# A message-passing layer on one core: PE one iteration free of ACT's evictions, and gathers that wait for the weights eight batches back

## The chip, the cores and the metric

The kernel runs on one core of one Trainium2 chip. The metric is the time of one execution on the device in microseconds (us). The engines are named as in the profile: PE (TensorE, matmuls), DVE (VectorE), ACT (ScalarE), POOL (GpSimd, which here issues the gathers) and SP (SyncE, which issues plain transfers). They run side by side and wait for each other by semaphores. SBUF is the memory that the engines work in, PSUM the banks that PE writes into.

## The reference

One layer of a graph network over 12500 nodes of 160 numbers (64 scalars and 32 vectors of three) and 400000 edges, which are sorted by their target node:

```python
h = jnp.maximum(_layernorm(x), 0.0)
s0, s1 = linear maps of h, times node_vec1          # the node's own part
y0, y1 = linear maps of h, times node_vec1          # what edges fetch
w = silu(edge_attr_16 @ fc_W1 / 4) @ fc_W2 / 8      # 192 weights of each edge: w_a, w_b, w_c, w_d
ys0, ys1 = y0[edge_src], y1[edge_src]               # the gather
e0, e1 = edge_attr_4[:, :1], edge_attr_4[:, 1:]
mid_a = w_a * ys0 * e0
mid_d = w_d * einsum('euc,ec->eu', ys1, e1) / sqrt(3)
mid_b = (w_b * ys0)[:, :, None] * e1[:, None, :]
mid_c = (w_c * e0)[:, :, None] * ys1
z = zeros.at[edge_dst].add(concatenated mids)       # 384 numbers of a node
out = x + C_S * s + C_X * (linear maps of z, times node_vec1)
```

## The kernel before, in words

A node phase of some 280 us computes s (into `acc`, which stays in SBUF) and y (written to `y_d` in HBM). Then come the edges, in 3125 tiles of 128, four tiles to a batch: 782 batches. This main loop is the rest of the time, and the change is in it.

The work on one batch, with its lines in the profile of the kernel before:

- `load`: POOL issues four indirect gathers (L540), one for each tile, that bring 128 rows of `y_d` each into one of nine buffers `yg`. The row numbers stand in `src_sb`. For 22 of the batches (every 32nd up to 704) no rows are gathered: `made_...` computes them from x, in small steps spread over the iterations before. So 760 batches are gathered, in 3037 instructions.
- `hidden` (every second batch): PE multiplies the edges' inputs into a bank `px` (L550), and ACT takes them out through Silu into `hT` (L555).
- `weigh`: PE's four fp32 matmuls write the batch's weights into one of two PSUM slots `pw` (L566); behind them ACT copies three numbers of each edge into the same slot (L567). This copy waits for the matmuls.
- `lift_rows`: ACT multiplies the fetched rows by e0 into `yge` (L484, four times).
- `dots_of` and `products`: DVE forms `tmp` (L489, L491), `both` (L495) and the product tile `pr` (L496, L497, L500, L501). L495 is the last to read the fetched rows on DVE. A `pw` slot is free for the batch after next when L501 has read it.
- `select` (once for 12 tiles): DVE compares a row of 0 to 127, kept in the free end of a bank `pz`, with the edges' targets, into the one-hot tile `sel` (L583).
- `sums`: PE adds sel^T pr of each tile (L603) into one of two banks `pz`.

Tiles form 185 groups, of 24 tiles in the first 1824 tiles and of 12 after. At a group's end ACT takes the sums out (`zs`, L609), PE transposes them into a `px` bank (`turn`, L617), ACT takes that out (`za`, L621), PE multiplies by the last weights (`map_sums`, L630), ACT takes that out (`os`, L634 and L635), and DVE adds it into `acc` (`accumulate`, L645 and L648).

PE, ACT and DVE run their instructions in exactly the order in which the program writes them; each takes the next only when what it waits for is there, and whatever stands behind it waits too. POOL has a queue of its own, also in program order, and so has SP. One iteration b of the loop writes: load(b+8), weigh(b+2), the evictions that PE's work of earlier iterations left for ACT, lift(b+2), dots and products of b+1, select, accumulate, sums(b), turn and map of groups due, and hidden. A turn is due one iteration after its group's last batch e, a map two, an accumulate four. A gather into a `yg` buffer may start when DVE and ACT have read the batch nine back, which had the buffer before.

Of the kernel before, what the change touches and what calls it, by code (L numbers as in the profile page):

```python
# [28 lines left out]
WN = 128  # L29
TG = 12  # L30
EG = 8
WIDE = 3, 5
GN = 8
HN = 2
RB = 22
RS = 32
# [7 lines left out]
def kernel(  # L44
# [56 lines left out]
    nr = max(0, min(RB, (NB - 1) // RS - 1))  # L101
# [3 lines left out]
    def made(b):  # L105

        return b // RS - 1 if b % RS == 0 and 0 < b <= nr * RS else None

# [26 lines left out]
    ygp = ctx.enter_context(tc.tile_pool(name="yg", bufs=9))  # L135
# [172 lines left out]
    with (  # L308
# [21 lines left out]
        def find_x():  # L330

            of = src_sb[:, RS * GT:RS * GT * (nr + 1)].rearrange("p (r c) -> p r c", c=RS * GT)[:, :, 0:GT]
            whole = nrp.tile([P, nr, GT], I32, name="whole")
            nc.vector.tensor_scalar(whole, of, 7, None, ALU.arith_shift_right)
            nc.vector.tensor_copy(hi_f.rearrange("p (r c) -> p r c", c=GT), whole)
            nc.vector.tensor_copy(lo_f.rearrange("p (r c) -> p r c", c=GT), of)
            nc.vector.scalar_tensor_tensor(lo_f, hi_f, -float(P), lo_f, op0=ALU.mult, op1=ALU.add)

        def gather_x(lo, hi):

            for r in range(lo, hi):
                xr = nrx.tile([P, GT * D + 1], F32, name="xr")
                for k in range(GT):
                    c = (r + 1) * RS * GT + k
# [141 lines left out]
    def dot(tmp, wt, yg, n):  # L486

        y1 = yg[:, :n, M0:].rearrange("p t (c u) -> p t c u", c=3)
        nc.vector.tensor_tensor(tmp[:, :n, 0:3, :], y1, wt[:, :n, NW:NW + 3].unsqueeze(3).to_broadcast([P, n, 3, M1]),  # L489
                                ALU.mult)  # L490
        nc.vector.tensor_reduce(tmp[:, :n, 3, :], tmp[:, :n, 0:3, :].rearrange("p t c u -> p t u c"), AX.X, ALU.add)  # L491

    def multiply(pr, both, tmp, wt, yg, yge, n):

        nc.vector.tensor_mul(both[:, :n, :], wt[:, :n, 96:160], yg[:, :n, 0:M0])  # L495
# [9 lines left out]
    with (  # L505
# [5 lines left out]
        tc.tile_pool(name="made", bufs=2) as mk,  # L511
        tc.tile_pool(name="banks", bufs=1, space=PSUM) as banks,
    ):
        (hids, rows, lifted, dots, wts, sels, z_ps, z_sb, zT, o_sb, prs) = ({} for _ in range(11))
        leaving = []
# [10 lines left out]
        AHEAD = 8  # L526
# [3 lines left out]

        def load(b):
            load_xe(b * GT // BT)
# [6 lines left out]
            for k, t in enumerate(tiles_of(b)):  # L539
                nc.gpsimd.indirect_dma_start(  # L540
                    out=yg[:, k, :], out_offset=None, in_=y_d,
                    in_offset=bass.IndirectOffsetOnAxis(ap=src_sb[:, t:t + 1], axis=0))
# [36 lines left out]
        def select(u, pz):  # L579
# [3 lines left out]
            nc.vector.tensor_tensor(sels[u][:, 0:n, :], pz[:, ZC:].unsqueeze(1).to_broadcast([P, n, WN]),  # L583
                                    drel[:, u * TG:u * TG + n].unsqueeze(2).to_broadcast([P, n, WN]), ALU.is_equal)
# [364 lines left out]
```

## Time and profile before

| What | Value |
|---|---|
| median of 3 runs | 5222.7 us (5202.25 to 5230.44) |
| profiled execution, its own time | 5204.84 us |
| its span in the profile | 5203.0 us |
| granted PE clock, share of full speed | 0.857 |

The profiled execution took 1.84 us beside its span. All times of single instructions come from it. In the views a line such as L540 is line 540 of the kernel; a name such as `yg<-y_d` is what an instruction writes and reads; a wait names the instruction that ended it, which is "issue" where the profile sees none.

### The profile page before, as it was taken

Reading aid. Unit: us, or ns where it says so; the run is one execution under the profiler, and the core shown is the slowest. Engines: PE = TensorE matmul, PEld = TensorE weight load, DVE = VectorE, ACT = ScalarE, POOL = GpSimd, SP = SyncE. Lnnn points to the kernel's source line nnn. Section 1 sums busy time; section 2 is a strip of 40 time slices with the busy share of each in tenths; the row PEclk is TensorE's granted clock in tenths of the full one; section 3 lists DMA queues with packets and bytes.
Section 4 is the critical chain, followed back from the end, with each engine's and each line's share of the span. In section 5 each row is a group of like instructions: output and inputs, shape, how many; then the busy total and the mean of one; then the engine's idle time right before and its main releaser. Section 6 shows DMA issues by size and latency. Waiting matters only on the chain. (4 is left out here: it accounts for less than half of the span.)

```text
span 5203.0 us, 55078 instructions
## 1 busy us (share of the span) xinstructions
PE 4180.4 (80%) x16329; PEld 2384.2 (46%) x16329; DVE 3441.9 (66%) x7529; ACT 1764.7 (34%) x5580; POOL 2959.6 (57%) x3137
## 2 busy tenths in 40 slices
PE   4478888787888888888888878888888888888888
PEld 3334444444444444444444444444444444544444
DVE  4456667666666666776666666676767666766667
ACT  3323333333333333332333333333333333333333
POOL 4455655555555555555555555555555555655553
PEclk7778888888888888888888888888888888888888
DMA  5322222222222222222222222222222222232222
GB/s 180 115 57 58 61 58 62 58 60 60 57 60 59 60 61 57 59 61 60 57 60 58 60 57 57 60 60 58 60 54 61 58 59 57 61 94 57 57 57 58
DMA packets 227720, 333.84 MB, mean 64 GB/s; under 512 B 54714, under 2 KB 171526, under 8 KB 227158
## 3 DMA queue, kind: packets, MB, share of 16 engines
q0 software_dynamic: 150000, 256.20, 19.9%
q1 hardware_dynamic: 63618, 65.63, 4.0%
q10 hardware_dynamic: 13796, 8.44, 0.5%
q8 instruction: 130, 2.13, 0.2%
q14 instruction: 176, 1.44, 0.1%
HBM read 306.83 MB, written 23.22 MB: 63 GB/s over the span
## 5 line engine op out<-in xcount | busy, mean ns | idle before, releaser
L540 POOL DMA_INDIRECT yg<-y_d,src_sb x3037 | 2871.3, 945 | 2115.7 <-ACT yge L484 784.9
L603 PE MATMUL pz<-pr,sel 128*128 128x384 f32 x6250 | 2510.0, 548 | 58.4 <-issue 54.7
L603 PEld LDWEIGHTS pz<-pr,sel 128*128 128x128 f32 x6250 | 1259.2, 212 | 1032.0 <-issue 491.5
L489 DVE TENSOR_TENSOR tmp<-yg,pw 128x384 f32<-128x384 f32 x760 | 418.6, 551 | 1523.1 <-ACT pw L567 1292.7
L567 ACT ACTIVATE pw<-raw 128x12 f32<-128x12 f32 x782 | 141.9, 182 | 3289.3 <-issue 2801.2
L484 ACT ACTIVATE yge<-yg,raw 128x160 f32<-128x160 f32 x3037 | 1044.0, 421 | 0.0
L566 PE MATMUL pw<-w,hT 64*128 64x192 f32 x6250 | 839.5, 392 | 73.7 <-issue 24.1
L566 PEld LDWEIGHTS pw<-w,hT 64*128 64x128 f32 x6250 | 572.6, 212 | 545.1 <-issue 313.4
L497 DVE TENSOR_TENSOR pr<-both,pw 128x768 f32<-128x768 f32 x782 | 737.9, 944 | 0.0
L550 PE MATMUL px<-xe,w 32*128 32x512 f32 x782 | 522.9, 756 | 189.4 <-ACT os L635 137.1
L491 DVE TENSOR_REDUCE tmp<-tmp 128x128 f32<-128x384 f32 x782 | 464.1, 594 | 26.9
L583 DVE TENSOR_TENSOR sel<-pz,drel 128x1536 f32<-128x1536 f32 (+1 forms) x261 | 455.2, 1744 | 0.0
L501 DVE TENSOR_TENSOR pr<-pw,yge 128x384 f32<-128x384 f32 x782 | 428.0, 547 | 0.0
L617 PE MATMUL px<-ident,zs 128*128 128x128 f32 x555 | 112.7, 319 | 358.9 <-ACT zs L609 341.3
L500 DVE TENSOR_TENSOR pr<-pw,yge 128x256 f32<-128x256 f32 x782 | 326.6, 418 | 13.0 <-ACT yge L484 12.3
L495 DVE TENSOR_TENSOR both<-pw,yg 128x256 f32<-128x256 f32 x760 | 314.8, 414 | 0.0
L550 PEld LDWEIGHTS px<-xe,w 32*128 32x128 f32 x782 | 130.7, 209 | 345.5 <-ACT os L635 163.4
L630 PE MATMUL px<-wc,za 128*128 128x96 f32 x1110 | 165.5, 289 | 145.3 <-ACT za L621 137.7
L617 PEld LDWEIGHTS px<-ident,zs 128*128 128x128 f32 x555 | 74.2, 159 | 446.9 <-ACT zs L609 395.9
L630 PEld LDWEIGHTS px<-wc,za 128*128 128x128 f32 x1110 | 161.5, 205 | 207.4 <-ACT za L621 155.1
L555 ACT ACTIVATE hT<-px 128x512 f32<-128x512 f32 x391 | 229.3, 587 | 1.9 <-PE px L550 1.7
L496 DVE TENSOR_TENSOR pr<-pw,tmp 128x128 f32<-128x128 f32 x782 | 219.4, 281 | 0.0
(118 smaller groups left out, 1739.2 us busy)
## 6 DMA issues: line engine op xcount, KB each, us to landing
yg<-y_d,src_sb POOLq DMA_INDIRECT x3037
xe<-in_e SPq DMA_DIRECT2D x196, 128.0 KB
y_d<-ys ACTq DMA_DIRECT2D x12, 640.0 KB
xr_d<-xr SPq DMA_DIRECT2D x22, 320.5 KB
acc<-in_x SPq DMA_DIRECT2D x11, 640.0 KB
xm<-xr_d SPq DMA_DIRECT2D x22, 320.0 KB
out<-acc SPq DMA_DIRECT2D x11, 640.0 KB
raw<-in_e SPq DMA_DIRECT2D x32, 192.0 KB
```

Source lines behind the costliest of these rows:

```text
L484: nc.scalar.activation(yge[:, k, :], yg[:, k, :], AF.Copy, scale=e4v[:, k, 0:1])
L489: nc.vector.tensor_tensor(tmp[:, :n, 0:3, :], y1, wt[:, :n, NW:NW + 3].unsqueeze(3).to_broadcast([P, n, 3, M1]), ALU.mult)
L491: nc.vector.tensor_reduce(tmp[:, :n, 3, :], tmp[:, :n, 0:3, :].rearrange("p t c u -> p t u c"), AX.X, ALU.add)
L497: nc.vector.tensor_mul(pr[:, :n, 192:ZC].rearrange("p t (c u) -> p t c u", c=3), both[:, :n, :].unsqueeze(2).to_broadcast([P, n, 3, M0]), ...
L500: nc.vector.tensor_mul(pr[:, :n, 0:M0], wt[:, :n, 0:M0], yge[:, :n, 0:M0])
L501: nc.vector.tensor_mul(pr[:, :n, 96:192].rearrange("p t (c u) -> p t c u", c=3), wt[:, :n, M0:96].unsqueeze(2).to_broadcast([P, n, 3, M1]) ...
L540: nc.gpsimd.indirect_dma_start(out=yg[:, k, :], out_offset=None, in_=y_d, in_offset=bass.IndirectOffsetOnAxis(ap=src_sb[:, t:t + 1], axis=0))
L550: nc.tensor.matmul(ph, w1[r, :], xe[r, :], start=True, stop=True)
L566: nc.tensor.matmul(pw[:, k, 0:NW], hT[r, o:o + P], w2[r, :], start=True, stop=True)
L583: nc.vector.tensor_tensor(sels[u][:, 0:n, :], pz[:, ZC:].unsqueeze(1).to_broadcast([P, n, WN]), drel[:, u * TG:u * TG + n].unsqueeze(2).to ...
L603: nc.tensor.matmul(z_ps[g], sels[t // TG][:, t % TG, :], pr[:, k, :], start=first, stop=last)
L630: nc.tensor.matmul(px[:, lo:hi], za[:, k, :], wc[:, k, lo:hi], start=k == 0, stop=k == 1)
```

## The change

1. A group's turn is due two iterations after its last batch, its map two or three after the turn (so that it falls on an odd iteration, while `hidden` uses a `px` bank on even ones), and its accumulate two after the map. The transposes go into the group's own `pz` bank instead of a `px` bank. At iteration b PE then needs only what ACT took out in iteration b-1, and a `px` bank is used at most once in an iteration.
2. The row of 0 to 127 for `select` is kept in four pieces of 32 in the free columns 224 to 255 of the `pw` slots, no longer in `pz`. `select` stands ahead of the products of its iteration, behind the dots.
3. `both` moves from `products` into `dots_of`, ahead of the reduction.
4. A new step `name_rows`: ACT copies the four row numbers of batch b+10 into a small tile `ids` (12 buffers), right behind the copy into `pw` of batch b+2. The gathers read `ids`; so those of batch j stand behind the weights of batch j-8. The gathers are written at the end of the iteration, ten batches ahead, and nine batches before the loop instead of eight. SP's load of edge inputs comes two batches earlier.
5. The 22 batches whose rows are computed lie elsewhere: every 24th in the part of wide groups (16), every 48th after (6), with the steps spaced 6 or 12 iterations apart.

On PE, about a third through its program, the end of a group and what follows it. `L603`/`L623` are the sums, `L566`/`L582` the weights of a batch; `L566` of the second list is `hidden`, and `L689`/`L709` belong to a computed batch. Before:

```order
L603 MATMUL pz_1673<-pr,sel 128x384 x4
L689 MATMUL px_1676<-ident,m_h 128x128 x2
L689 MATMUL px_1676<-ident,m_oh 128x128
L566 MATMUL pw_1671<-w_99,hT 128x192 x4
L603 MATMUL pz_1674<-pr,sel 128x384 x4
L617 MATMUL px_1675<-ident,zs 128x128 x3
L550 MATMUL px_1676<-xe,w_98 128x512
L566 MATMUL pw_1672<-w_99,hT 128x192 x4
L603 MATMUL pz_1674<-pr,sel 128x384 x4
L630 MATMUL px_1675<-wc,za 128x96
```

After:

```order
L623 MATMUL pz_1679<-pr,sel 128x384 x4
L709 MATMUL px_1681<-ident,m_h 128x128 x2
L709 MATMUL px_1681<-ident,m_oh 128x128
L582 MATMUL pw_1676<-w_99,hT 128x192 x4
L623 MATMUL pz_1678<-pr,sel 128x384 x4
L566 MATMUL px_1680<-xe,w_98 128x512
L582 MATMUL pw_1677<-w_99,hT 128x192 x4
L623 MATMUL pz_1678<-pr,sel 128x384 x4
L637 MATMUL pz_1679<-ident,zs 128x128 x3
```

The transposes of a group (L617, now L637) stood ahead of the second batch of weights behind the group's end, and now stand behind it and the sums that follow it. They write `pz_1679`, the group's own bank; before it was a `px` bank, whose other one `hidden` took right behind.

On ACT, also at the end of a group: the copy into `pw` (L567, now L583) and what stands behind it. Before:

```order
L567 ACTIVATE pw_1671<-raw 128x4x3
L609 ACTIVATE zs<-pz_1673 128x384
L693 ACTIVATE m_t<-px_1676 128x384
L484 ACTIVATE yge<-yg,raw 128x160 x4
L567 ACTIVATE pw_1672<-raw 128x4x3
```

After (L545 is the copy of row numbers):

```order
L583 ACTIVATE pw_1676<-raw 128x4x3
L545 ACTIVATE ids<-src_sb 128x4
L629 ACTIVATE zs<-pz_1678 128x384
L713 ACTIVATE m_t<-px_1681 128x384
L493 ACTIVATE yge<-yg,raw 128x160 x4
L583 ACTIVATE pw_1677<-raw 128x4x3
```

Behind each copy into `pw` there is now the copy of row numbers, ahead of the evictions and the lifts.

On POOL, in the middle of its program, a batch's four gathers and the first of the next, with the semaphores that each waits for. Before:

```order
L540 DMA yg<-y_d,src_sb 128x160 [waits DMASW0_49,DVE_49,Activation_49]
L540 DMA yg<-y_d,src_sb 128x160 [waits DMASW1_49]
L540 DMA yg<-y_d,src_sb 128x160 [waits DMASW2_49]
L540 DMA yg<-y_d,src_sb 128x160 [waits DMASW3_49]
L540 DMA yg<-y_d,src_sb 128x160 [waits DMASW4_49,DVE_49,Activation_49]
```

After:

```order
L555 DMA yg<-y_d,ids 128x160 [waits DMASW0_49,DVE_49,Activation_49]
L555 DMA yg<-y_d,ids 128x160 [waits DMASW1_49]
L555 DMA yg<-y_d,ids 128x160 [waits DMASW2_49]
L555 DMA yg<-y_d,ids 128x160 [waits DMASW3_49]
L555 DMA yg<-y_d,ids 128x160 [waits DMASW4_49,DVE_49,Activation_49]
```

The first gather of a batch waits for DVE and ACT in both. What moved is the ACT instruction: before it is the lift of the batch that had the buffer, now it is the copy into the batch's `ids`.

The diff, without the parts that only rename or fit the search for the computed batches' nodes:

```diff
 GT = 4
 BT = 32
 WN = 128
+SP = 256 - WN // 4
 TG = 12
 EG = 8
+YB = 9
 WIDE = 3, 5
 GN = 8
 HN = 2
-RB = 22
-RS = 32
+RB = 16, 6
+RS = 24, 48
 LO = D - P
 EPS = 1e-5
 C_S = math.sin(math.pi / 8.0)
...
     dram = ctx.enter_context(tc.tile_pool(name="dram", bufs=1, space=DRAM))
     y_d = dram.tile([N, D], F32, name="y_d")
-    nr = max(0, min(RB, (NB - 1) // RS - 1))
+    n1 = max(0, min(RB[0], wide // GT // RS[0] - 2, (NB - 1) // RS[0] - 1))
+    from2 = wide // GT // RS[0] * RS[0] + RS[1]
+    n2 = max(0, min(RB[1], (NB - 1 - from2) // RS[1] + 1))
+    made_at = [RS[0] * (r + 2) for r in range(n1)] + [from2 + RS[1] * r for r in range(n2)]
+    nr = n1 + n2
     RT = nr * GT
     xr_d = dram.tile([max(nr, 1) * P, GT * D + 1], F32, name="xr_d")
     def made(b):
-        return b // RS - 1 if b % RS == 0 and 0 < b <= nr * RS else None
+        return made_at.index(b) if b in made_at else None
     z_d = dram.tile([ZR, ZC], F32, name="z_d")
...
         for k in range(n):
             nc.scalar.activation(yge[:, k, :], yg[:, k, :], AF.Copy, scale=e4v[:, k, 0:1])
-    def dot(tmp, wt, yg, n):
+    def dot(tmp, both, wt, yg, n):
         y1 = yg[:, :n, M0:].rearrange("p t (c u) -> p t c u", c=3)
         nc.vector.tensor_tensor(tmp[:, :n, 0:3, :], y1, wt[:, :n, NW:NW + 3].unsqueeze(3).to_broadcast([P, n, 3, M1]),
                                 ALU.mult)
+        nc.vector.tensor_mul(both[:, :n, :], wt[:, :n, 96:160], yg[:, :n, 0:M0])
         nc.vector.tensor_reduce(tmp[:, :n, 3, :], tmp[:, :n, 0:3, :].rearrange("p t c u -> p t u c"), AX.X, ALU.add)
-    def multiply(pr, both, tmp, wt, yg, yge, n):
-
-        nc.vector.tensor_mul(both[:, :n, :], wt[:, :n, 96:160], yg[:, :n, 0:M0])
+    def multiply(pr, both, tmp, wt, yge, n):
+
         nc.vector.tensor_mul(pr[:, :n, M0:96], wt[:, :n, 160:NW], tmp[:, :n, 3, :])
         nc.vector.tensor_mul(pr[:, :n, 192:ZC].rearrange("p t (c u) -> p t c u", c=3),
                              both[:, :n, :].unsqueeze(2).to_broadcast([P, n, 3, M0]),
...
             return pxs[turns["px"] % 2]
         K = TG // GT
-        AHEAD = 8
+        AHEAD = YB + 1
         def tiles_of(b):
             return list(range(b * GT, min((b + 1) * GT, T)))
+        def name_rows(b):
+            if made(b) is None:
+                ids[b] = idp.tile([P, GT], I32, name="ids")
+                n = len(tiles_of(b))
+                nc.scalar.activation(ids[b][:, :n], src_sb[:, b * GT:b * GT + n], AF.Copy)
+
         def load(b):
-            load_xe(b * GT // BT)
             r = made(b)
             if r is not None:
                 rows[b] = xms[r]
...
             for k, t in enumerate(tiles_of(b)):
                 nc.gpsimd.indirect_dma_start(
                     out=yg[:, k, :], out_offset=None, in_=y_d,
-                    in_offset=bass.IndirectOffsetOnAxis(ap=src_sb[:, t:t + 1], axis=0))
+                    in_offset=bass.IndirectOffsetOnAxis(ap=ids[b][:, k:k + 1] if b in ids else src_sb[:, t:t + 1],
+                                                        axis=0))
         def hidden(s):
...
             o = g % EG * TG + k * GT
             return raws[g // EG][:, o:o + GT, :]
-        def select(u, pz):
+        def select(u, pw):
             n = min(TG, T - u * TG)
             sels[u] = selp.tile([P, TG, WN], F32, name="sel")
-            nc.vector.tensor_tensor(sels[u][:, 0:n, :], pz[:, ZC:].unsqueeze(1).to_broadcast([P, n, WN]),
-                                    drel[:, u * TG:u * TG + n].unsqueeze(2).to_broadcast([P, n, WN]), ALU.is_equal)
+            for_each = pw[:, :, SP:].unsqueeze(1).to_broadcast([P, n, GT, WN // GT])
+            nc.vector.tensor_tensor(sels[u][:, 0:n, :].rearrange("p t (k c) -> p t k c", k=GT), for_each,
+                                    drel[:, u * TG:u * TG + n].unsqueeze(2).unsqueeze(3).to_broadcast(
+                                        [P, n, GT, WN // GT]), ALU.is_equal)
         def dots_of(b):
-            dots[b] = part.tile([P, GT, 4, M1], F32, name="tmp")
-            dot(dots[b], wts[b], rows[b], len(tiles_of(b)))
+            tmp = part.tile([P, GT, 4, M1], F32, name="tmp")
+            both = part.tile([P, GT, M0], F32, name="both")
+            dot(tmp, both, wts[b], rows.pop(b), len(tiles_of(b)))
+            dots[b] = tmp, both
         def products(b):
             pr = prod.tile([P, GT, ZC], F32, name="pr")
-            both = part.tile([P, GT, M0], F32, name="both")
-            multiply(pr, both, dots.pop(b), wts.pop(b), rows.pop(b), lifted.pop(b), len(tiles_of(b)))
+            tmp, both = dots.pop(b)
+            multiply(pr, both, tmp, wts.pop(b), lifted.pop(b), len(tiles_of(b)))
             prs[b] = pr
         def sums(b):
...
         def turn(g):
             zs = z_sb.pop(g)
-            pt = next_px()[:, 0:3 * P].rearrange("p (k c) -> p k c", k=3)
+            pt = pzs[g % 2][:, 0:3 * P].rearrange("p (k c) -> p k c", k=3)
             for k in range(3):
                 nc.tensor.transpose(pt[:, k, :], zs[:, P * k:P * (k + 1)], ident)
...
         def plan(r):
-            end = (r + 1) * RS - 9
+            b = made_at[r]
+            step, lag = (6, 2) if b * GT <= wide else (12, 6)
+            end = b - 7 - lag
             last = end - (end + 1) % 6
-            first = last - 6 * (GT - 1)
+            first = last - step * (GT - 1)
             for when, b, f in ([(at_start, first - 6, made_load), (on_vector, first - 3, made_moments),
                                 (on_vector, first - 1, made_reciprocal)]):
                 when.setdefault(max(b, 0), []).append(lambda f=f: f(r))
             for k in range(GT):
-                j = first + 6 * k
-                for when, b, f in ((on_vector, j - 1, made_rows), (on_tensor, j, made_turn), (on_tensor, j + 2, made_map),
-                                   (on_vector, j + 4, made_attr), (on_scalar, j + 5, made_leave)):
+                j = first + step * k
+                for when, b, f in ((on_vector, j - 1, made_rows), (on_tensor, j, made_turn), (on_tensor, j + lag, made_map),
+                                   (on_vector, j + lag + 2, made_attr), (on_scalar, j + lag + 3, made_leave)):
                     when.setdefault(b, []).append(lambda f=f, k=k: f(r, k))
         for r in range(nr):
...
         order = tc.manual_schedule(engines={mybir.EngineType.PE, mybir.EngineType.Activation, mybir.EngineType.DVE})
         with order:
             e4_load(0)
-            for b in range(min(AHEAD, NB)):
+            for blk in range(min(AHEAD - 1, NB - 1) * GT // BT + 1):
+                load_xe(blk)
+            for b in range(min(YB, NB)):
                 load(b)
             relate_edges(0, part, lim)
             for s in range(3):
...
                 all_leave()
             if NQ == 1:
                 any_far(next_px()[0:1, 0:1])
+            for pw in pws:
+                nc.vector.tensor_copy(pw[:, :, SP:], iota[:, 0:WN].rearrange("p (k c) -> p k c", k=GT))
             for b in range(min(2, NB)):
                 weigh(b)
                 lift_rows(b)
-            for pz in pzs:
-                nc.vector.tensor_copy(pz[:, ZC:], iota[:, 0:WN])
             dots_of(0)
+            if YB < NB:
+                load(YB)
+            select(0, wts[0])
             products(0)
-            select(0, pzs[0])
             last_batch = [(t - 1) // GT for t in ends]
             turns_at, maps_at, adds_at = {}, {}, {}
             for g, e in enumerate(last_batch):
-                turns_at.setdefault(e + 1, []).append(g)
-                maps_at.setdefault(e + 2, []).append(g)
-                adds_at.setdefault(e + (4 if e + 4 < NB else 3), []).append(g)
+                at_end = e + 4 >= NB
+                t = e + (1 if at_end else 2)
+                m = t + (1 if at_end else 2 if (t + 2) % 2 else 3)
+                turns_at.setdefault(t, []).append(g)
+                maps_at.setdefault(m, []).append(g)
+                adds_at.setdefault(m + (1 if at_end else 2), []).append(g)
             for b in range(NB + 3):
                 u, k = divmod(b, K)
                 due(at_start, b)
                 if b + AHEAD < NB:
-                    load(b + AHEAD)
+                    load_xe((b + AHEAD) * GT // BT)
                 if b < NB:
                     q, r = divmod(b, EG * K)
                     if r == 0:
...
                         any_far(next_px()[0:1, 0:1])
                 if b + 2 < NB:
                     weigh(b + 2)
+                if b + AHEAD < NB:
+                    name_rows(b + AHEAD)
                 all_leave()
                 due(on_scalar, b)
                 if b + 2 < NB:
                     lift_rows(b + 2)
                 if b + 1 < NB:
                     dots_of(b + 1)
+                    if k == K - 1:
+                        select(u + 1, wts[b + 1])
                     products(b + 1)
-                    if k == K - 1:
-                        select(u + 1, pzs[(group_at[b * GT] + 1) % 2])
+                if b + AHEAD < NB:
+                    load(b + AHEAD)
                 for g in adds_at.get(b, []):
                     accumulate(g)
                     leave_before(g + 1)
```

More of the change, by code (lines that the diff above doesn't have):

```diff
@@ L863 @@
                 tmp = fp.tile([P, GT, 4, M1], F32, name="f_tmp")
[L864 removed]
                 pr = fp.tile([P, GT, ZC], F32, name="f_pr")
                 both = fp.tile([P, GT, M0], F32, name="f_both")
[L867 removed]
+                dot(tmp, both, pw, yg, GT)
+                multiply(pr, both, tmp, pw, yge, GT)
                 for k in range(GT):
```

18 lines of the change are left out of this document (10 added, 8 removed).

## The prediction

> **What bounds the kernel now.** I read the page first: its busy shares, then its costliest groups.
>
> ```profile
> PE 4180.4 (80%) x16329; PEld 2384.2 (46%) x16329; DVE 3441.9 (66%) x7529; ACT 1764.7 (34%) x5580; POOL 2959.6 (57%) x3137
> ...
> L540 POOL DMA_INDIRECT yg<-y_d,src_sb x3037 | 2871.3, 945 | 2115.7 <-ACT yge L484 784.9
> ...
> L567 ACT ACTIVATE pw<-raw 128x12 f32<-128x12 f32 x782 | 141.9, 182 | 3289.3 <-issue 2801.2
> ...
> L583 DVE TENSOR_TENSOR sel<-pz,drel 128x1536 f32<-128x1536 f32 (+1 forms) x261 | 455.2, 1744 | 0.0
> ```
>
> No engine is full. L567, a copy of 0.18 us behind each batch's four weight matmuls, has 3289 us of idle time ahead of it. So the next view is that of the waits (engine, tile and line that waited, what ended it, us in total, times, longest):
>
> ```profile
> ACT pw L567 <- issue: 2801.2, 542, 31.7
> DVE tmp L489 <- ACT pw L567: 1314.1, 298, 29.8
> POOL yg L540 <- ACT yge L484: 784.9, 235, 10.4
> ...
> POOL yg L540 <- ACT pw L567: 161.0, 40, 8.2
> POOL yg L540 <- ACT zs L609: 154.3, 35, 5.0
> ...
> PE px L617 <- ACT zs L609: 341.3, 82, 9.7
> PE px L630 <- ACT za L621: 137.7, 27, 9.8
> ...
> POOL yg L540 <- ACT xm L720: 28.4, 8, 4.2
> ...
> POOL yg L540 <- ACT hT L555: 26.9, 7, 4.8
> ```
>
> The five POOL rows are its real pauses: 784.9 + 161.0 + 154.3 + 28.4 + 26.9 = 1155.5 us in 325 pauses, 3.56 us each. (The ACT instruction named is whatever ran last; by the program POOL waits there for DVE's read of a buffer.) A gather takes 0.945 + 0.30 us of issue, so 3037 take 3796 us. Span 5203.0 - 3796 - 1155 leaves 252 us, mostly the node phase's share. In the main loop POOL is thus always gathering or paused, and the pauses are what can move.
>
> Why it pauses shows in the timeline (start, duration, idle before in brackets), between 5110 and 5132 us:
>
> ```profile
> 5110.27 0.94 POOL L540 DMA_INDIRECT yg<-y_d,src_sb  x1 [7.61 <-ACT yge L484]
> ...
> 5114.22 0.92 PE L566 MATMUL pw<-w,hT 64*128 64x192 f32 x8
> ...
> 5115.24 0.18 ACT L567 ACTIVATE pw<-raw 128x12 f32<-128x12 f32 x1 [4.03 <-DVE both L495]
> ...
> 5118.18 0.92 PE L566 MATMUL pw<-w,hT 64*128 64x192 f32 x8
> ...
> 5124.03 0.95 POOL L540 DMA_INDIRECT yg<-y_d,src_sb  x1 [0.30 <-issue]
> 5127.17 0.18 ACT L567 ACTIVATE pw<-raw 128x12 f32<-128x12 f32 x1 [9.59 <-issue]
> 5127.29 0.47 ACT L621 ACTIVATE za<-px 128x384 f32<-128x384 f32 x1
> 5127.39 0.56 DVE L489 TENSOR_TENSOR tmp<-yg,pw 128x384 f32<-128x384 f32 x1 [6.80 <-ACT pw L567]
> ...
> 5128.48 0.42 DVE L495 TENSOR_TENSOR both<-pw,yg 128x256 f32<-128x256 f32 x1
> ...
> 5129.64 0.94 POOL L540 DMA_INDIRECT yg<-y_d,src_sb  x1 [4.67 <-ACT yge L484]
> ...
> 5130.21 0.55 DVE L501 TENSOR_TENSOR pr<-pw,yge 128x384 f32<-128x384 f32 x1
> ...
> 5131.34 1.65 PE L566 MATMUL pw<-w,hT 64*128 64x192 f32 x8
> ```
>
> POOL gathers without a pause from 5110.27. Weights that end at 5115.14, 4.87 us into this run of gathers, are seen by ACT at once (5115.24). Weights that end at 5119.10, 8.83 us into it, are seen only at 5127.17, 2.19 us after POOL's last gather has ended (5124.98). POOL had run out of batches it may fetch: the next needs the `both` of the held batch (L495). I call this a hold. Then come L489, L491 and L495, ending at 5128.90, and 0.74 us later POOL goes on: 2.47 us after L567. Pause: 2.19 + 2.47 = 4.66 us.
>
> I set all 782 weight groups against their copies, by how far into a run of gathers the matmuls ended, and call a copy over 2 us late held. The first of those under 6 us, and first and last of those of 8 us and more:
>
> ```profile
> 289.30 1.65 PE L566 MATMUL pw<-w,hT 64*128 64x192 f32 x8 [2.84 <-DVE pr L501]
> ...
> 291.04 0.18 ACT L567 ACTIVATE pw<-raw 128x12 f32<-128x12 f32 x1 [2.13 <-PE pw L566]
> ...
> 225.92 2.93 PE L566 MATMUL pw<-w,hT 64*128 64x192 f32 x16
> ...
> 227.62 0.18 ACT L567 ACTIVATE pw<-raw 128x12 f32<-128x12 f32 x1 [0.99 <-PE pw L566]
> ```
>
> The last of 8 us and more is that of 5118.18 above; the last under 6 us stands with the third rival. Held were 53 of 405 under 6 us (14 of the 134 between 3 and 6), 33 of 97 between 6 and 8, 181 of 190 from 8 on. Of the 243 copies over 4 us late, 91% came after the run's last gather, the median 2.38 us after it. So a long run of gathers holds up PE's signal, and the run's end frees it.
>
> **The change part by part.**
>
> *Gathers behind the copy of row numbers.* A gather of batch j now waits for the copy that stands behind the weights of batch j-8, no longer for `both` of j-9. Two effects.
> First, in a hold POOL resumes sooner after L567 is through. The copy would start 0.12 us after it (as L621 at 5127.29 does) and take 0.18 (L567's own 128x12), so it ends 0.30 us after; POOL reacts 0.74 us after its cause (5128.90 to 5129.64), or at the least as fast as DVE, whose L489 starts 0.04 after L567's end. Bounds: 0.34 and 1.04 us, against 2.47. I take 0.9, near POOL's own row. With 2.3 us between the last gather and the release (2.19 here, 2.38 the median) a pause is 3.2 us instead of 4.7.
> Second, POOL runs out one batch sooner in a hold, so a hold lasts up to 5 us (four gathers) less. I count that only through the number of pauses.
> The Trainium skill, "SBUF — State Buffer", Who interferes with whom, speaks against the first part of this: PE and ACT never wait on anyone, and only DVE and GpSimd share a pair of ports. It is a rule on ports, not on signals, and the trace (181 of 190 held) shows ACT waiting while GpSimd gathers; by the rule alone the holds would stay as they are, and the time at about 5205 of the profiled execution's own.
>
> The 760 copies cost ACT 760 x 0.182 = 138 us. Upper bound: all of it in the time. ACT is 34% busy and DVE waits for its lifts nowhere that the rows above show, so I take 0; the cover is ACT's idle time ahead of L567.
>
> *PE an iteration free.* Transposes and maps come one and up to two iterations later and the transposes stay in their own bank. The waits of 341.3 and 137.7 us (L617, L630) lie inside holds: at 5127.29 L621 left only after L567. Their own gain lies between 0 and 479 us; I take 0, since PE is freed into the same hold. What they change is that PE can do the next batch's weights within the hold. So two copies come at the release, the second about 1.6 us after the first (rows 5151.30 and 5152.93 below, where this happened already).
>
> *Batches per pause.* Time from the release of batch m. DVE needs 5127.17 to 5130.76, 3.6 us, until the bank of m is free; weights m+2 end 0.2 + 0.92 to 1.65 later, at 4.7 to 5.4. Gathers began at 0.9, so this is 3.8 to 4.5 us into the run: in 9 of 10 cases not held. Batch m+1 takes DVE 3.4 us more (5127.39 to 5130.76), and in one of three `select` (1.74) stands ahead of its products; weights m+3 end between 8.1 and 10.5, 7.2 to 9.6 into the run: mostly held. So three batches per pause. The same reckoning for before gives two (4.87 and 8.83 above); the trace has 760 / 325 = 2.34.
>
> *Sum.* 760 gathered batches / 3 = 253 pauses x 3.2 = 810 us against 1155.5: -345. With the bounds 0.34 and 1.04 for POOL's start: 253 x 2.64 = 668 (-488) and 253 x 3.34 = 845 (-310).
>
> *The rest.* `select` moved ahead of products: 261 x 1.74 = 455 us of DVE as before; bound 0 to 455 if all of it delayed the weights; taken as 0 beyond the reckoning above, covered by PE's spare iteration. `both` ahead of the reduce: the same instructions, -0.6 to 0 us a pause; no longer what POOL waits for, so 0. The batches made on chip keep their number (22) and work; other dates, 0; bound: one wrongly placed step each holds PE for an eviction, 88 x 0.47 (L621) = 41 us. Two more batches ahead of the loop: 10 us of gathers (2 x 4 x 1.25) beside preparation, 0 to 10; taken as 0. SP's load of edge data two batches earlier: 0.
>
> The profiled execution took 5204.84 us, 17.9 under the median of 5222.7. 5204.84 - 345 = 4860; on the median's scale **4878**.
>
> **The rivals.**
>
> 1. *Two batches per pause.* Weights m+2 are held too, because the shorter pause leaves the next run less room. 760 / 2 = 380 pauses x 3.2 = 1216: +60, 5283 on the median's scale. For it: 33 of 97 held already between 6 and 8 us, where a `select` could push m+2. Against: 14 of 134 at the place reckoned.
>
> 2. *Long runs.* With weights always ready, most signals come early enough and five batches pass per pause: 152 x 3.2 = 486, -669: 4553. For it: 2.34 where the reckoning gave 2. Against: 181 of 190 from 8 us on.
>
> 3. *Short pauses do not clear it (slower).* Before, a pause was mostly 4 to 5 us. The signal may need a long one:
>
> ```profile
> 5146.20 0.92 PE L566 MATMUL pw<-w,hT 64*128 64x192 f32 x8
> 5146.75 0.94 POOL L540 DMA_INDIRECT yg<-y_d,src_sb  x1 [1.49 <-ACT yge L484]
> ...
> 5150.88 0.92 PE L566 MATMUL pw<-w,hT 64*128 64x192 f32 x8
> 5151.30 0.18 ACT L567 ACTIVATE pw<-raw 128x12 f32<-128x12 f32 x1 [4.82 <-issue]
> 5152.93 0.17 ACT L567 ACTIVATE pw<-raw 128x12 f32<-128x12 f32 x1
> ```
>
> After a pause of 1.49 us weights were held from 0.37 us into the run on. If 3.2 us clear as little, only the pair passes, every second time one batch: 1.5 per pause, 507 x 3.2 = 1622, +467: 5690. It decides from 2.1 batches per pause down (760 / 2.1 x 3.2 = 1158). Against: with all pauses taken together, only 39 of the 271 weights in the first 3 us of a run were held.
>
> 4. *The hold has another cause* and the gathers only wait in its shadow, or gathers still wait as before: then ACT's 2801 us stay and POOL only waits elsewhere: about 5223, between 5085 (L630's 137.7 us gone, by PE's spare iteration) and 5361 (the 138 us of copies in the time). Against: the release 2.38 us after the last gather. The rule of the Trainium skill's "SBUF — State Buffer" named above would end here.
>
> **How the numbers follow.** Three batches per pause (2.4 to 4) 0.47, 4700 to 5060; long runs 0.18; two per pause 0.14; 1.5 per pause 0.06; another cause 0.15, of which 0.03 faster, 0.06 the same, 0.06 slower. About 0.5% can be told from no change here. Faster 0.47 + 0.18 + 0.03 = 0.68, same 0.06, slower 0.14 + 0.06 + 0.06 = 0.26. The range 4560 to 5300 leaves out rival 3 (0.06), half of the long runs (0.09) and a few of rival 1 (0.03). The predicted time is that of the likeliest; its own range is 4700 to 5060.
>
> **What would show it.** Right: POOL's waits name the copies of row numbers, some 250 of about 3.2 us; two copies into `pw` within 2 us after most pauses; runs of 12 gathers the commonest; PE's waits for `zs` and `za` near nothing; ACT's idle time ahead of `pw` down by some 345 us. Wrong: runs of 8 (rival 1), 4 to 8 (rival 3), 20 and more (rival 2), or copies late at any place of a run (rival 4). The forecast fails most easily if the weights m+2 fall later into the run than 6 us.

## The result and the profile after

The changed kernel took 4777.2 us (median of 4 runs, 4772.0 to 4782.2) against 5218.4 us before (median of 4): 0.9159 of the time, 95% interval 0.9136 to 0.9181. The forecast was 4878.

The page of the changed kernel, its busy shares and the groups that answer to those shown of before:

```profile
PE 4061.2 (85%) x16329; PEld 2320.6 (49%) x16329; DVE 3410.0 (71%) x7531; ACT 1819.5 (38%) x6330; POOL 2967.2 (62%) x3137
...
L555 POOL DMA_INDIRECT yg<-y_d,ids x2997 | 2842.2, 948 | 1612.5 <-issue 782.1
...
L583 ACT ACTIVATE pw<-raw 128x12 f32<-128x12 f32 x782 | 139.8, 179 | 2802.8 <-issue 1190.0
...
L545 ACT ACTIVATE ids<-src_sb 128x4 int32<-128x4 int32 x750 | 143.0, 191 | 0.2
```

The work is the same (16329 matmuls, 2997 gathers here and 40 of the first batches in a row of their own). The idle time of ACT ahead of the copy into `pw` fell from 3289.3 to 2802.8 us, and the new copies of row numbers, 143 us of ACT, did not show in the time. The waits of the changed kernel:

```profile
POOL yg L555 <- ACT ids L545: 739.1, 259, 7.3
...
PE pz L623 <- ACT za L641: 57.5, 50, 3.6
...
PE pz L637 <- ACT zs L629: 11.2, 16, 1.1
...
PE px L650 <- ACT za L641: 4.6, 3, 2.4
```

POOL's pauses are now 739.1 us in 259, 2.85 us each, against 1155.5 in 325, 3.56 each; a few waits of POOL under other names (`pw`, `yge`, `za`, `hT`) add 13 us. So the pauses that these rows name fell by some 403 us, and the profiled execution by 5204.84 - 4772.01 = 433. The rest lies in pauses whose end the profile does not name. The rows of POOL under `issue`, before and after:

```profile
POOL yg L540 <- issue: 782.1, 2292, 3.5
...
POOL yg L555 <- issue: 794.0, 2567, 2.1
```

Most of these are the 0.30 us between two gathers, but before, the longest is 3.5 us, and 63 gaps of over 0.6 us, 98.1 us in all, stand there; after, 16 of 14.6 us. Counting every gap of over 0.6 us between two gathers, under whatever name, the kernel before has 366 pauses of 1246.6 us (3.41 each) and the changed kernel 279 of 782.0 us (2.80 each): 465 less. Shorter gaps took 23 us more and the gathers themselves 9 us more, which leaves the 433. PE's waits for `zs` and `za`, 479 us before, are 73.

One cycle of the changed kernel in the timeline:

```profile
2501.29 0.18 ACT L583 ACTIVATE pw<-raw 128x12 f32<-128x12 f32 x1 [10.08 <-remote]
2501.41 0.19 ACT L545 ACTIVATE ids<-src_sb 128x4 int32<-128x4 int32 x1
...
2501.87 0.95 POOL L555 DMA_INDIRECT yg<-y_d,ids  x1 [2.79 <-ACT ids L545]
...
2503.53 0.17 ACT L583 ACTIVATE pw<-raw 128x12 f32<-128x12 f32 x1
...
2504.94 0.92 PE L582 MATMUL pw<-w,hT 64*128 64x192 f32 x8 [1.62 <-DVE pr L510]
...
2505.96 0.18 ACT L583 ACTIVATE pw<-raw 128x12 f32<-128x12 f32 x1 [0.38 <-issue]
...
2511.31 0.92 PE L582 MATMUL pw<-w,hT 64*128 64x192 f32 x8
...
2515.58 0.92 PE L582 MATMUL pw<-w,hT 64*128 64x192 f32 x8
2515.63 0.95 POOL L555 DMA_INDIRECT yg<-y_d,ids  x1 [0.30 <-issue]
...
2518.97 0.18 ACT L583 ACTIVATE pw<-raw 128x12 f32<-128x12 f32 x1 [10.79 <-remote]
...
2519.54 0.94 POOL L555 DMA_INDIRECT yg<-y_d,ids  x1 [2.97 <-ACT ids L545]
2520.94 0.16 ACT L583 ACTIVATE pw<-raw 128x12 f32<-128x12 f32 x1
```

At 2501.29 a held copy comes through, and POOL goes on 0.58 us later. The second copy, whose weights were ready too, follows at 2503.53. The third batch's weights end at 2505.86, 4.0 us into the run of gathers, and are seen at once. Those of the fourth end at 2512.23, 10.4 us into it, and are held until 2518.97, 2.39 us after POOL's last gather (which ends at 2516.58); by then the weights of the fifth wait as well. Twelve gathers, three batches, make the run. Over the whole execution 209 of 280 runs have 12 gathers, 46 have 8, 21 have 4 and two have 16. In the median the first copy into `pw` of a pause starts 2.30 us after the last gather, and the second copy 2.13 us after the first: within 2 us at 90 of the 279 pauses, within 2.5 us at 244. Sorted as in the prediction, copies over 2 us late are 28 of 241 below 6 us into a run, 34 of 80 from 6 to 8, and 305 of 309 from 8 on.

### The profile page after: what moved, and what is told of

Read it like the earlier page. It is cut to its first block, busy times and chain, and to the rows that moved or that the text cites. A ratio compares the mean times of both kernels' runs of the same rounds, so it can differ in the third digit from the quotient of the medians.

```text
span 4770.2 us, 55691 instructions
## 1 busy us (share of the span) xinstructions
PE 4061.2 (85%) x16329; PEld 2320.6 (49%) x16329; DVE 3410.0 (71%) x7531; ACT 1819.5 (38%) x6330; POOL 2967.2 (62%) x3137
## 4 chain that ended last, share of the span: by engine, by line
PE 25%; another core or an unknown queue 23%; issue 22%; DVE 18%; ACT 10%; DMA 1%; ACTq 0%; DVEq 0%; POOL 0%; SPq 0%; POOLq 0%
PE pz L623 15%; PE pw L582 6%; ACT yge L493 5%; DVE pr L506 3%; DVE tmp L498 3%; DVE tmp L501 2%; PE px L566 2%; DVE pr L510 2%; DVE pr L509 2%; DVE both L500 2%; ACT pw L583 1%; DVE pr L505 1%; DVE sel L600 1%; ACT hT L571 1%
## 5 line engine op out<-in xcount | busy, mean ns | idle before, releaser
L555 POOL DMA_INDIRECT yg<-y_d,ids x2997 | 2842.2, 948 | 1612.5 <-issue 782.1
L623 PE MATMUL pz<-pr,sel 128*128 128x384 f32 x6250 | 2529.9, 549 | 143.5 <-issue 83.9
L623 PEld LDWEIGHTS pz<-pr,sel 128*128 128x128 f32 x6250 | 1253.0, 211 | 1130.3 <-issue 550.7
L583 ACT ACTIVATE pw<-raw 128x12 f32<-128x12 f32 x782 | 139.8, 179 | 2802.8 <-issue 1190.0
L582 PE MATMUL pw<-w,hT 64*128 64x192 f32 x6250 | 825.8, 368 | 388.6 <-DVE pr L510 238.9
L582 PEld LDWEIGHTS pw<-w,hT 64*128 64x128 f32 x6250 | 546.8, 196 | 780.5 <-issue 416.3
L566 PE MATMUL px<-xe,w 32*128 32x512 f32 x782 | 444.2, 650 | 35.2 <-ACT hT L571 20.4
L600 DVE TENSOR_TENSOR sel<-pw,drel 128x1536 f32<-128x1536 f32 (+1 forms) x261 | 454.8, 1743 | 0.0
L566 PEld LDWEIGHTS px<-xe,w 32*128 32x128 f32 x782 | 115.2, 184 | 240.1 <-issue 152.3
L650 PE MATMUL px<-wc,za 128*128 128x96 f32 x1110 | 153.4, 275 | 6.1 <-ACT za L641 4.6
L668 DVE SCALAR_TENSOR_TENSOR acc<-os,by,acc 128x160 f32 x370 | 143.4, 388 | 14.4 <-ACT os L655 1.0
L545 ACT ACTIVATE ids<-src_sb 128x4 int32<-128x4 int32 x750 | 143.0, 191 | 0.2
```

Source lines behind the costliest of these rows:

```text
L555: nc.gpsimd.indirect_dma_start(out=yg[:, k, :], out_offset=None, in_=y_d, in_offset=bass.IndirectOffsetOnAxis(ap=ids[b][:, k:k + 1] if b i ...
L566: nc.tensor.matmul(ph, w1[r, :], xe[r, :], start=True, stop=True)
L582: nc.tensor.matmul(pw[:, k, 0:NW], hT[r, o:o + P], w2[r, :], start=True, stop=True)
L600: nc.vector.tensor_tensor(sels[u][:, 0:n, :].rearrange("p t (k c) -> p t k c", k=GT), for_each, drel[:, u * TG:u * TG + n].unsqueeze(2).un ...
L623: nc.tensor.matmul(z_ps[g], sels[t // TG][:, t % TG, :], pr[:, k, :], start=first, stop=last)
```

## The experiments

Every kernel was run beside the kernel before on the same chip. That kernel's median differed from chip to chip (5259, 5278 and 5221 us), so the comparisons go by ratios; the changed kernel's is 0.916. Where pauses are counted below, a pause is again a gap of over 0.6 us between two gathers, unless a row is named.

**The gate alone.** The kernel before, with the copies of row numbers and the gathers ten batches ahead:

```diff
+        def name_rows(b):
+            if made(b) is None:
+                ids[b] = idp.tile([P, GT], I32, name="ids")
...
                     weigh(b + 2)
+                if b + AHEAD < NB:
+                    name_rows(b + AHEAD)
                 all_leave()
```

> The kernel before with one part of the change: ACT's copies of row numbers behind the copy into pw, gathers reading them, written ten batches ahead. Turns, maps, banks, both and select stay as before. Theory (a long run of gathers holds PE's signal to ACT until the run ends): a pause shrinks from 4.7 to 2.9 us (2.3 to the release, 0.6 to the next gather), but only one copy is ready at a release, since PE still stands at the transposes or maps; the next weights come in time, the ones after them are held: two batches per pause, 380 x 2.9 = 1100 us of pauses against 1155. Time 5000 to 5220, near 5165, runs of 8 gathers the commonest. Rival (the gate is what gains, PE's freedom is not needed): three batches per pause, 4780 to 4850.

Measured: 0.9324 (0.9294 to 0.9354). The waits of this kernel (L536 is its copy of row numbers, L616 and L628 take out `zs` and `za`):

```profile
POOL yg L546 <- ACT ids L536: 834.0, 321, 8.3
...
PE px L624 <- ACT zs L616: 204.1, 76, 6.4
PE px L637 <- ACT za L628: 196.1, 61, 5.5
```

Neither range was met (0.9324 of 5218 us is 4866). The gate carries by far the larger part, 6.8 of 8.4 points. The row of `ids` names 321 pauses of 2.60 us. All pauses are 374 of 2.50 us, 933 us in all, against 366 of 3.41 us before. So two batches pass per pause, as expected (380 pauses), and runs of 8 are the commonest (174 of 375). What was too long is the pause, 2.9 us, and what was too small is the sum of before, 1155 us, which leaves out pauses. A second copy follows the first within 2.5 us at 107 of the 374 pauses, against 244 of 279 in the changed kernel.

**PE's freedom alone.** The changed kernel with gathers reading the row numbers where they lie:

```diff
-            if made(b) is None:
+            if False:
                 ids[b] = idp.tile([P, GT], I32, name="ids")
```

> The changed kernel without the copies of row numbers: gathers read the row numbers where they lie, and wait for both of the batch nine back. PE's free iteration stays. Theory: two copies per release, as changed; POOL goes on behind both, some 1.9 us after the copy into pw instead of 0.6, and a pause is 4.2 us; three to three and a half batches per pause: 223 to 253 pauses, 940 to 1060 us against the 740 of the changed kernel. Time 4980 to 5100. Rival (PE's freedom alone gains, the gate does nothing): 4777 within 25 us.

Measured: 0.9897 (0.9863 to 0.9931). Its waits, and a release in its timeline:

```profile
POOL yg L555 <- ACT pw L583: 1055.2, 222, 10.7
...
POOL yg L555 <- ACT yge L493: 74.4, 71, 10.3
...
POOL yg L555 <- ACT zs L629: 56.0, 8, 10.1
```

```profile
2515.72 0.18 ACT L583 ACTIVATE pw<-raw 128x12 f32<-128x12 f32 x1 [10.85 <-remote]
...
2516.31 1.37 ACT L493 ACTIVATE yge<-yg,raw 128x160 f32<-128x160 f32 x4
2516.40 0.42 DVE L500 TENSOR_TENSOR both<-pw,yg 128x256 f32<-128x256 f32 x1
2517.59 0.16 ACT L583 ACTIVATE pw<-raw 128x12 f32<-128x12 f32 x1
2517.95 0.94 POOL L555 DMA_INDIRECT yg<-y_d,src_sb  x1 [4.67 <-ACT pw L583]
```

0.9897 of 5218 us is 5165, above the range that I gave. Pauses become fewer (278 instead of 366; 223 to 253 were expected) but longer: 4.42 us each, and 4.75 us for the 222 of the first row, instead of the 4.2 expected. The rows show why: `both` of the released batch ends at 2516.82, but POOL goes on at 2517.95, 0.27 us after the batch's lifts (2516.31 + 1.37 = 2517.68). The buffer has two readers, and with `both` moved ahead of the reduce the lift on ACT is the later one. Fewer but longer pauses come to 1229 us, nearly the 1247 of before.

**The distance.** Gathers eight batches ahead, so that those of batch j stand behind the weights of j-6:

```diff
-        AHEAD = YB + 1
+        AHEAD = YB - 1
...
-            for b in range(min(YB, NB)):
+            for b in range(AHEAD - 1):
                 load(b)
...
```

> The changed kernel with gathers written eight batches ahead instead of ten, so that those of batch j stand behind the weights of batch j-6 instead of j-8. Theory: at each release POOL is at the end of what it may fetch, whatever the distance, so runs and pauses stay the same: 4777 within 25 us (0.5%). Rival (the distance sets how long a hold lasts: ten us less a hold): 4500 to 4700. Second rival (six batches are too few, DVE waits for rows): over 4830, with waits of DVE for the gathers.

Measured: 0.9151 (0.9127 to 0.9175), the changed kernel's ratio. The row of `ids` names 266 pauses, 813.1 us in all, and there is no wait of DVE for rows worth naming (0.5 us). That it is eight does not matter; POOL is at the end of what it may fetch at every release either way.

**No gathers.** POOL gathers nothing in the edge loop; SP brings consecutive rows:

```diff
-                nc.gpsimd.indirect_dma_start(
...
+            r = b % 23 * GT * P
+            nc.sync.dma_start(yg[:, :n, :], y_d[r:r + n * P, :].rearrange("(t p) c -> p t c", p=P))
```

> The changed kernel in which POOL gathers nothing in the edge loop: SP brings 512 consecutive rows of y_d into the buffer of each batch by one plain transfer, so the rows are not those that the edges name; everything else is computed alike, the copies of row numbers included. Theory: without runs of gathers ACT sees the weights at once: over 90% of the copies into pw within 0.3 us of free weights, and the time falls by the pauses of 740 us and more, to 4050 to 4300, where PE (4061 us busy) bounds. Rival (the held copies have another cause than the gathers): late copies stay, 4650 to 4800.

Measured: 3760.7 us beside 5259 of before in a single run, below the range that I gave. That range took PE's 4061 us as the bound; PE was busy for 3616 us here, at a granted clock of 0.982 instead of 0.904. Busy shares and the waits of ACT and DVE of this kernel:

```profile
PE 3616.4 (96%) x16329; PEld 2137.9 (57%) x16329; DVE 3398.0 (90%) x7531; ACT 1844.9 (49%) x6330; POOL 88.5 (2%) x100
```

```profile
ACT pw L581 <- issue: 1636.5, 705, 3.3
...
DVE tmp L498 <- ACT pw L581: 162.2, 258, 3.9
```

Not one of the 782 copies starts over 1 us after both its weights and ACT's instruction before are done; in the changed kernel 318 do, in the kernel before 287. ACT still waits for weights, but 3.3 us at most, since it is simply ahead of PE. So the held copies come with the gathers. The run changes two things at once, the gathers and the kind of transfer; it shows that the kernel without the gathers has no holds, not what in a gather does it.

**`select` back behind the products.**

```diff
-                    if k == K - 1:
-                        select(u + 1, wts[b + 1])
+                    held = wts[b + 1]
                     products(b + 1)
+                    if k == K - 1:
+                        select(u + 1, held)
```

> The changed kernel with select behind the products again, as before (it still reads the row of 0 to 127 from pw). Theory: a third of the batches get their weights up to 1.7 us sooner after a release, so some copies that were held come through: 4720 to 4790. Rival (the place of select matters as it was changed, since the products' slot stays taken by it): over 4800.

Measured: 0.9153 (0.9137 to 0.9168), no difference to the changed kernel's 0.9159 (0.9153 of 5218 us is 4776, in the range, but the gain that the theory spoke of can't be told). The place of `select` costs and gains nothing that can be told: runs of 12 stay the commonest (211 of 283).

**Dates of turn, map and accumulate as before**, all else as changed:

```diff
-                t = e + (1 if at_end else 2)
-                m = t + (1 if at_end else 2 if (t + 2) % 2 else 3)
+                t = e + 1
+                m = e + 2
                 turns_at.setdefault(t, []).append(g)
                 maps_at.setdefault(m, []).append(g)
-                adds_at.setdefault(m + (1 if at_end else 2), []).append(g)
+                adds_at.setdefault(e + (3 if at_end else 4), []).append(g)
```

> The changed kernel with the dates of before for turn (e+1), map (e+2) and accumulate (e+4); transposes stay in the group's own bank, the gate stays. Theory: where a group ends or is mapped in a hold, PE stands there and the second copy is not ready at the release, as in the run with the gate alone; a part of the 1.8% between that run and the changed kernel comes back: 4800 to 4865, with more pauses than 259 and waits of PE for zs and za. Rival (PE's free iteration is worth nothing beside the gate): 4777 within 20 us.

Measured: 0.9339 (0.9324 to 0.9355), the ratio of the gate alone. Its waits:

```profile
POOL yg L555 <- ACT ids L545: 842.1, 332, 7.5
...
PE px L650 <- ACT za L641: 223.9, 67, 4.9
PE pz L637 <- ACT zs L629: 198.8, 66, 6.1
```

The row of `ids` names 332 pauses instead of 259 (361 instead of 279 in all), and PE waits for `zs` and `za` again. So the dates are worth 1.8 points with the gate in place, 2.0% of the changed kernel's time, a little more than the 0.5 to 1.8% expected; banks, `select`, `both` and the other places of the computed batches together are worth nothing that these runs can tell (0.9339 against 0.9324).

**The copy of row numbers behind the lifts**, one step moved on ACT:

```diff
-                if b + AHEAD < NB:
-                    name_rows(b + AHEAD)
                 all_leave()
                 due(on_scalar, b)
                 if b + 2 < NB:
                     lift_rows(b + 2)
+                if b + AHEAD < NB:
+                    name_rows(b + AHEAD)
```

> The changed kernel with the copy of row numbers moved on ACT from right behind the copy into pw to behind the four lifts of the same iteration. Theory (the gate gains because POOL goes on 0.57 us after the released copy, and not behind the lifts of the held batch): a pause grows by the evictions and lifts, 1.5 to 2 us, to 4.4 to 4.8 us; 250 pauses x 1.5 to 2 = 375 to 500 us more, 0.985 to 1.010 of the kernel before. Rival (the gate gains by something else: the distance of eight, or POOL waiting for ACT alone): within 2% of the changed kernel, 0.90 to 0.935 of the kernel before.

Measured: 0.9922 (0.9892 to 0.9953), nearly all of the gain gone, as forecast (268 pauses of 4.54 us). A release of this kernel:

```profile
2527.20 0.18 ACT L583 ACTIVATE pw<-raw 128x12 f32<-128x12 f32 x1 [10.71 <-remote]
...
2529.08 0.19 ACT L545 ACTIVATE ids<-src_sb 128x4 int32<-128x4 int32 x1
2529.17 0.16 ACT L583 ACTIVATE pw<-raw 128x12 f32<-128x12 f32 x1
2529.53 0.95 POOL L555 DMA_INDIRECT yg<-y_d,ids  x1 [4.96 <-ACT pw L583]
```

The copy comes 1.88 us after the released one, POOL 0.26 us behind it: a pause of 4.96 us, 2.33 us after the released copy instead of 0.58. So the gate's gain is where it stands on ACT, right behind the released copy.

**Does other work of POOL let the signals through?** Three kernels, none of which could answer.

```diff
                         axis=0))
+            nc.gpsimd.memset(mark, 0.0)
```

> The changed kernel with one small memset (128x1) on POOL behind the four gathers of every batch. Theory (what counts is for how long gathers go on; only some 2.3 us without gathers let PE's signals through): the memset's 0.06 to 0.3 us break nothing, holds and pauses stay, runs of 12 gathers with gaps of under 0.7 us inside; time 4777 plus 760 x 0.1 to 0.35: 4850 to 5040. Rival (any instruction of POOL that is not a gather lets the signals through): no run is longer than four gathers, copies come within 0.3 us, time 4150 to 4400.

> The changed kernel with six memsets of 128x480 on POOL (some 2.9 us) behind every second batch's gathers: POOL gathers for at most 10 us, then does other work and does not wait. Theory (the absence of gathers frees the signals, not POOL's standing at a wait): weights are seen at the latest 2.3 us after the eighth gather, POOL hardly waits for row numbers, copies over 4 us late nearly vanish; time 3796 + 390 x 3 + 250 = 5200 or so (5100 to 5300). Rival (POOL must stand at a wait for the signals to pass): holds and pauses stay beside the memsets: 5700 to 6000.

The second had six memsets of 128x480 behind every second batch. Measured, a single run each: 4895.0 beside 5278 (0.927), and 5664.2 beside 5278. POOL's order is not among those that the program fixes, and the memsets wait for nothing, so they were moved: in the first all 760 lie before 1000 us, in the second they stand behind every batch in the first part of the loop and nowhere after some 3400 us. Where they stood in the second, POOL needed 8.2 us a batch and DVE waited for rows:

```profile
DVE tmp L498 <- DMA yg<-y_d,ids: 1334.3, 363, 20.3
```

The third tied them to the row numbers:

```diff
...
+            if b in ids and b % 2:
+                for _ in range(28):
+                    nc.gpsimd.memset(ids[b][:, GT:], 0)
```

> The changed kernel with 28 small memsets on POOL tied to the row numbers of every second batch (the copy of row numbers takes one column more, and the memsets write that column), so that some 20 to 24 of them stand behind every eight gathers: POOL does 2 to 4 us of other work there, without waiting for ACT. The memsets of the two runs before had no such tie, were moved elsewhere in POOL's queue and could tell nothing. Theory (the absence of gathers frees PE's signals, not POOL's standing at a wait): held copies start some 2 us after the eighth gather, while POOL is in its memsets, and POOL's waits for row numbers nearly vanish (under 200 us); time 3796 + 250 + 380 x 28 x 0.11 to 0.16 = 5200 to 5750. Rival (POOL must stand at a wait): copies stay held through the memsets, POOL's waits for row numbers stay near 740 us on top: over 5900.

Measured: 5764.1 us beside 5221 in a single run. POOL's waits for row numbers are 11.8 us, and only 5 copies are held by the measure used above (over 1 us late), which speaks for the theory. But POOL is now so slow that DVE waits 1954.2 us for rows and ACT's lifts wait too, so hardly any weights are ready while gathers run long (22 of 782 end 6 us or more into a run): whether POOL must stand at a wait, or only not gather, stays open.

## Why the prediction was right, point by point

*The hold.* A long run of gathers holds PE's signal, and its end frees it: confirmed by the kernel without gathers (no held copy of 782), and seen again after (305 of 309 from 8 us on, the release 2.30 us after the last gather in the median). The trace also records when a semaphore is raised. At 277 of the 279 copies of the changed kernel that start over 2 us after their weights with ACT idle for over 1 us, PE's is recorded within 0.2 us ahead of the copy (before: 235 of 240; in the hold of the prediction at 5127.10, for weights that ended at 5119.10). So it is the signal that comes late, not ACT that sees it late. How a gather holds a signal is not shown by any run. The rule of the Trainium skill's "SBUF — State Buffer", Who interferes with whom, is that PE and ACT never wait on anyone, and it stands there for ports. The trace differs from it where it is read more widely: ACT stood idle, its weights done, until the gathers stopped.

*The pause.* Forecast 3.2 us, measured 2.85 by the row of `ids`. The release was right (2.3 forecast, 2.30 the median). The mis-sized term is POOL's start after the released copy: I took 0.9 us between 0.34 and 1.04, near POOL's reaction of 0.74 us to DVE, and it is 0.58: POOL starts 0.27 us after the end of ACT's copy, in 262 of the 263 pauses of over 1.5 us.

*The sum.* -345 fell short of -433 by 88 us. Of these, 58 are the pauses that the rows name: 810 us forecast, 739 and 13 measured. The other 30 come from the start of the sum: I took the five rows for all of POOL's pauses, and 63 more stood under `issue` in the kernel before. By all gaps, 366 pauses before passed 760 / 366 = 2.1 batches each, the two that the reckoning gave, and not 2.34; and the 279 after of 2.80 us come to 782 us, against the 253 of 3.2 us, 810 us, of the forecast. The count was too low and the length too long, and that the two nearly cancel is luck. A reading in the third rival was wrong as well: before, 102 of the 366 pauses were of 4 to 5 us and 208 were shorter.

*Three batches per pause.* 760 / 259 = 2.93 (2.7 by all 279), with runs of 12 the commonest, as forecast. In the cycle shown, weights of the third batch came 4.0 us into the run and of the fourth 10.4; in the median of the runs of 12, the first weights to end in a run come at 4.7 us (3.8 to 4.5 forecast) and the second at 9.9 (7.2 to 9.6 forecast). One sign was not met: two copies within 2 us after most pauses. The second copy comes 2.13 us after the first in the median, and I took 1.6 from one place of the trace.

*Which part does what.* Here the working was less good than its sum. I put the fall in the number of pauses down to PE's free iteration and was right (361 to 279 with the gate, 366 to 278 without). But I thought that the gate would give little without it (near 5165): alone the gate gives 6.8 of the 8.4 points, by shorter pauses at about the same number. And PE's freedom needs the gate: alone it gives 1.0 point, since each pause then lasts 4.42 us. One part sets the count of the pauses, the other their length. The step "the next needs the `both` of the held batch" was incomplete: the lift of that batch holds the buffer as well, and is the later of the two once `both` is moved ahead.

*Costs set to nothing.* The copies (143 us of ACT), `select` and the computed batches cost nothing that the runs can tell, as taken; only `select` was measured alone. The distance of eight, of which I counted nothing, is worth nothing against six.

*The rivals.* Two batches per pause: 46 runs of 8 against 209 of 12. Long runs: two of 16. Short pauses that do not clear: of the 64 weights in the first 4 us behind pauses of 2.4 to 3.2 us none was held over 2 us; behind pauses of 0.6 to 1 us, 11 of 12 in the first 2 us were. So a pause can be too short, but not one that lasts until the signal is through. Another cause: excluded by the kernel without gathers, with the limit told there.

## What to carry to other kernels

Where an engine waits for a signal that is long due, look at what every other engine does when it is released; a time that repeats (here 2.3 us after the last gather) names the cause better than the wait's own row. If a stall can't be removed, make what ends it short: the instruction that lets the stalled queue go on belongs directly behind the released one, ahead of all that merely became possible (1.88 us of evictions and lifts were worth 7.6 points here). Count and length of stalls multiply, so two parts of a change are measured alone and together before either is called useless. And count stalls by the gaps themselves, not only by the rows that name a releaser: 98 us of pauses stood under `issue` here.

## What the runs showed of the hardware that was not expected

POOL went on 0.27 us after the end of an ACT instruction that it waited for (262 of 263 pauses of over 1.5 us in the changed kernel), but 0.74 us after one of DVE (252 of the 294 such pauses of the kernel before lie 0.7 to 0.8 us behind the end of `both`). The two differ in more than the engine: in the kernel before, POOL waits for DVE in an instruction of its own ahead of the gather, which ends at 5128.94 in the hold of the prediction, 0.70 us before the gather starts, while the gather itself waits for ACT. Which of the two makes the difference is not shown.

The granted PE clock rose with fewer holds, 0.857 before, 0.904 after and 0.982 without gathers, and PE's busy time for the same 16329 matmuls fell from 4180 to 4061 and 3616 us. The sum of the prediction had no term for it, and all of the 433 us are found in POOL's gaps and gathers; in the kernel without gathers, where PE is busy for 96% of the span, PE's busy time taken as unchanged is why the expectation was too high.
